# Layer 0 of a graph transformer: two PSUM banks become one region that scores, weights and picks share in turn

## The chip, the cores and the metric

The kernel runs on one core of one Trainium2 chip. A core has five engines that work side by side, each through its own queue in order: PE (TensorE, matmuls; PEld is its weight load), DVE (VectorE), ACT (ScalarE), POOL (GpSimd) and SP (SyncE, which here only issues DMAs). PE writes its results into PSUM, which has eight banks of 128 partitions x 512 fp32 values, and DVE or ACT copy them out. The metric is the device time of one execution in microseconds (us), lower is better.

## The reference

Three layers of graph attention over 6250 nodes of 64 features and 206250 edges that are sorted by target node; then a log-softmax, a residual and a layer norm:

```python
q = x @ Wq + bq;  k = x @ Wk + bk;  v = x @ Wv + bv
e = edge_attr @ We
alpha = sum(q[dst] * (k[src] + e)) / sqrt(64)          # one score per edge
p = exp(alpha - segment_max(alpha, dst)[dst])
w = p / segment_sum(p, dst)[dst]
agg = segment_sum((v[src] + e) * w, dst)
x = relu(agg + x @ Ws + bs)                            # layers 0 and 1: then a layer norm
```

## The kernel before, in words

Edges are cut into chunks of 768 (six tiles of 128), and four chunks make a unit: 67 full units and a rest. A unit's edges meet only a few target nodes, 32 for each chunk, so its scores are one 128 x 768 matrix: four groups of 32 rows (one for each chunk) by 768 edges, computed in two halves of 384 columns.

For a unit, each layer does this:
- **Gather.** The features of each edge's source node are needed. Most come by indirect DMA (POOL, L607). Some tiles come from PE instead, as *picks*: edges are sorted so that a tile's sources lie in known windows of nodes, and a matmul of a one-hot matrix `hot` (made on DVE from keys, L1342) with the node features `parts` picks them out (L1404, eight matmuls of 256 columns for one tile of two chunks). Each pick gives four candidates side by side in PSUM. DVE copies the first out (L1365) and overwrites it with the second, third and fourth where a mask says so (L1367, three `COPY_PREDICATED`). This is `evacuate()`. A later `swap()` on ACT (L1353 to L1355) exchanges lower halves between the two chunks.
- **Turn.** Features are transposed on PE (L1705) and copied by ACT to `featT` (L1708), one chunk in each quarter of the unit.
- **Scores** (`products`, L1718): PE multiplies `featT` with the queries. **Most** (L1732): DVE adds the mask and keeps the row maximum. **Powers** (L1751): ACT takes the exponential over both halves. **Weights** (L1765): PE transposes the result, three tiles for each half, and ACT copies it out (L1768). **Sums** (L1777): PE multiplies the weights with the features, and ACT copies the result out (L1784).

Layer 0 has a second job beside this, the sorter: it brings the edges of each unit into the order that the picks need. A unit of sorting is 12 steps, called by `move(n)`. Each step makes two `hit` matrices on DVE (L1081) for the step after next, prepares a third of the edge data on DVE (L1049 or L1052), and does six matmuls with them on PE (L1092), in half of the steps four more (L1101), with transposes (L1135) in four of the steps. Every fourth unit a `mark` runs beside it for about two units: it computes the positions of the next 16 chunks, almost all on DVE (L916 to L1017) with a few matmuls (L930, L949, L951, L977, L1006). A group of 512 nodes that is complete is finished and projected for the next layer in small pieces at the start of units (for instance L1449 on PE, L1451 on DVE, L1554 on PE, L1557 on DVE).

The order on each engine is the order in which the loop over units writes the instructions; nothing reorders it. In one pass `u` of that loop, unit `u` is turned quarter by quarter (`j` = 0 to 3), unit `u-1` gets scores, most, powers and weights, unit `u-2` gets sums, and picks are made for unit `u+1`. With eight tiles from picks a unit of layer 0 has four picks, one in each quarter: two sorter steps, the pick, one more step, `evacuate()`.

PSUM in layer 0 before: tag `a` has two banks (transposes and the sorter's small things), `x` two (the sorter's products), `g`, `m`, `s` and `p` one each. Bank `s` holds scores half 0, scores half 1, the pick of quarter 1 and the pick of quarter 2 in turn. Bank `p` holds the pick of quarter 0, weights half 0, weights half 1 and the pick of quarter 3. Each tenant starts when the last has been read out. Layers 1 and 2 have other pools (opened after layer 0), where picks already come in doubles, with copies of 256 columns, in two buffers of two banks.

In the listings the same work has other numbers after the change: scores L1723 for L1718, most L1737 for L1732, the negated maximum L1750 for L1745, powers L1756 for L1751, weights L1776 for L1765, probT L1779 for L1768, sums L1788 for L1777. Lines up to L1404 keep theirs.

## Time and profile before

| what | value |
|---|---|
| median of 3 runs | 4164.22 us (4156.0 to 4164.31) |
| the profiled execution | 4160.32 us, of which the span is 4158.5 us |
| PE busy | 3390.2 us (82%) |
| DVE busy | 3094.5 us (74%) |
| POOL busy | 2819.2 us (68%) |
| ACT busy | 2344.7 us (56%) |
| mean granted clock of PE | 0.925 |

A row of the timeline gives the start (us from the span's start), the time of the group (us), engine, line, operation, output<-inputs with partitions x elements, the count, and in brackets how long the engine sat idle before it and what ended that. Starts of PE's matmuls are denser than their times, since they are pipelined. A row of the windows gives a stretch, its length, and the busy time and instructions of PE, PEld, DVE, ACT and POOL in it, then the granted clock, the share of the DMA engines and GB/s.

### The profile page before, as it was taken

The page shows a single profiled execution, that of the slowest core. Times are in us where ns is not written, and L with a number is a line of the kernel's source. Part 1 is how long each engine was busy: PE and PEld are TensorE (multiplying, and loading weights), DVE is VectorE, ACT ScalarE, POOL GpSimd, SP SyncE. Part 2 cuts the span into 40 slices and gives each one's busy share as a digit, 9 for nine tenths or more (in the row PEclk, how much of TensorE's full clock was granted, in tenths as well). Part 3 has the DMA queues.
Part 4 walks back from the last instruction along what each step waited for, and adds up shares of the span by engine and source line. Part 5 has one row for each costly group of instructions (what it writes and reads, how often), then busy time and mean ns, then how long its engine had stood idle before and what let it go on. Part 6 is the DMA issues. An engine that isn't in the chain of part 4 may idle for free.

```text
span 4158.5 us, 105258 instructions
## 1 busy us (share of the span) xinstructions
PE 3390.2 (82%) x34183; PEld 2406.9 (58%) x34183; DVE 3094.5 (74%) x10306; ACT 2344.7 (56%) x5994; POOL 2819.2 (68%) x2774
## 2 busy tenths in 40 slices
PE   3779988998999899995778788888758788787776
PEld 2345555555555555553666666666646666666664
DVE  5678888888888888874566677677646767777775
ACT  1345555555565565563555556665535666666665
POOL 5466666666666666663777777777747777777774
PEclk9889999999999999996899999999969999999997
DMA  5657676667667767675677777777657677777774
GB/s 120 165 163 194 175 186 177 168 181 185 174 176 186 181 174 187 171 199 137 151 181 185 189 191 188 185 190 197 167 129 183 176 185 186 185 185 190 185 185 100
DMA packets 787997, 728.88 MB, mean 175 GB/s; under 512 B 487336, under 2 KB 612450, under 8 KB 787440
## 3 DMA queue, kind: packets, MB, share of 16 engines
q1 hardware_dynamic: 630436, 504.14, 47.5%
q0 software_dynamic: 88448, 90.75, 11.8%
q10 hardware_dynamic: 68556, 127.16, 8.6%
q8 instruction: 278, 4.55, 0.5%
q14 instruction: 279, 2.29, 0.2%
HBM read 562.78 MB, written 158.81 MB: 174 GB/s over the span
## 4 chain that ended last, share of the span: by engine, by line


## 5 line engine op out<-in xcount | busy, mean ns | idle before, releaser
L607 POOL DMA_INDIRECT feat<-x,gate x1592 | 1568.8, 985 | 485.3 <-issue 367.3
L607 POOL DMA_INDIRECT feat<-in_x,gate x1100 | 1177.7, 1071 | 676.0 <-ACT gate L639 360.8
L1404 PE MATMUL ps_x<-parts,hot 128*128 128x256 f32 x6336 | 942.5, 301 | 0.0
L1404 PEld LDWEIGHTS ps_x<-parts,hot 128*128 128x128 f32 x6336 | 842.2, 202 | 82.2 <-DVE feat L1367 65.6
L1708 ACT COPY featT<-ps_a 64x384 f32<-64x384 f32 x1320 | 626.7, 475 | 410.3 <-PE ps_a L1705 392.7
L1367 DVE COPY_PREDICATED feat<-which,ps_x 128x256 f32<-128x256 int32 (+1 forms) x1584 | 592.8, 374 | 54.3
L1365 DVE COPY feat<-ps_x 128x256 f32<-128x256 f32 (+1 forms) x528 | 187.8, 356 | 580.8 <-PE ps_x L1404 564.9
L1705 PE MATMUL ps_a<-ident,feat 128*128 128x128 f32 x2380 | 450.2, 290 | 145.2 <-DMA feat<-x,gate 107.0
L1705 PEld LDWEIGHTS ps_a<-ident,feat 128*128 128x128 f32 x2380 | 285.1, 145 | 354.1 <-issue 261.1
L1081 DVE TENSOR_SCALAR hit<-ruler,pos 128x384 bf16<-128x384 f16 x1608 | 457.3, 326 | 7.3 <-PE ps_m L1101 6.6
L1342 DVE TENSOR_SCALAR hot<-keys,rank 128x512 fp32r<-128x512 f16 (+1 forms) x1040 | 432.7, 483 | 5.4 <-DMA keys<-keyS 5.4
L1777 PE MATMUL ps_p<-feat,probT 128*32 128x128 f32 x6600 | 242.8, 300 | 84.6 <-ACT probT L1768 73.8
L1092 PE MATMUL ps_x<-hit,raw 128*64 128x384 bf16 x1608 | 296.0, 364 | 0.5 <-DVE hit L1081 0.4
L1092 PE MATMUL ps_x<-hit,rest 128*64 128x384 bf16 x1608 | 277.8, 342 | 0.0
L1092 PE MATMUL ps_x<-hit,end 128*64 128x384 bf16 x1608 | 277.3, 341 | 0.0
L1777 PEld LDWEIGHTS ps_p<-feat,probT 128*32 128x32 f32 x6600 | 198.9, 122 | 123.2 <-ACT probT L1768 98.2
L1718 PE MATMUL ps_s<-featT,q 128*32 128x384 f32 x1866 | 235.2, 509 | 32.6 <-DVE most L1732 25.4
L1765 PE MATMUL ps_s<-ident,prob 128*128 128x128 f32 (+1 forms) x417 | 83.4, 313 | 215.4 <-ACT prob L1751 214.3
L1751 ACT ACTIVATE prob<-prob,part 128x768 f32<-128x768 f32 x204 | 190.0, 932 | 83.8 <-DVE part L1745 75.5
L1125 ACT COPY eT<-ps_x 128x384 f32<-128x384 f32 x268 | 129.3, 483 | 122.5 <-PE ps_x L1092 89.6
L1765 PEld LDWEIGHTS ps_s<-ident,prob 128*128 128x128 f32 (+1 forms) x417 | 47.8, 152 | 245.9 <-ACT prob L1751 241.5
L1143 ACT COPY feat<-ps_a 128x384 f32<-128x384 f32 x256 | 122.1, 481 | 120.6 <-PE ps_a L1135 89.7
(280 smaller groups left out, 6019.1 us busy)
## 6 DMA issues: line engine op xcount, KB each, us to landing
featT<-eaS SPq DMA_DIRECT2D x658, 192.0 KB
feat<-eaP SPq DMA_DIRECT2D x134, 768.0 KB
raw<-in_ea SPq DMA_DIRECT2D x536, 96.0 KB
eaS<-eT ACTq DMA_DIRECT2D x134, 384.0 KB
keys<-keyS SPq DMA_DIRECT2D x132, 384.0 KB
eaP<-feat ACTq DMA_DIRECT2D x128, 384.0 KB
shade<-maskS SPq DMA_DIRECT2D x198, 192.0 KB
fourth<-eaS SPq DMA_DIRECT2D x134, 192.0 KB
```

Source lines behind the costliest of these rows:

```text
L607: nc.gpsimd.indirect_dma_start(out=feat[:, c, t, 0], out_offset=None, in_=xts[layer][:, :], in_offset=bass.IndirectOffsetOnAxis(ap=index[: ...
L1081: nc.vector.tensor_scalar(hit, ruler, self.pos[:, at : at + 1], None, ALU.is_equal)
L1092: nc.tensor.matmul(self.px[j * D : (j + 1) * D, :HE], self.parts[2 * h + i].thirds[part][:, j, t * D : (t + 1) * D], self.hits[h, 2 * i + ...
L1342: nc.vector.tensor_scalar(hot[:, h], keys[self.layer, k][:, first : first + n], rank[:, h : h + 1], None, ALU.is_equal)
L1365: nc.vector.tensor_copy(found, px[:, :, :, 0])
L1367: nc.vector.copy_predicated(found, which[:, :, :, b].bitcast(I32).unsqueeze(3).to_broadcast([P, 2, m, D]), px[:, :, :, b],)
L1404: nc.tensor.matmul(px[:, t - t0, v].rearrange("p b d -> p (b d)"), hot[:, h, (2 * pair + v) * P : (2 * pair + v + 1) * P], those[:, i, b0 ...
L1705: nc.tensor.transpose(pt[:, t * P : (t + 1) * P], rows[:, 2 * t * D : 2 * (t + 1) * D], ident)
L1708: nc.scalar.copy(featT[:, :, h, :], pt[h * D : (h + 1) * D, : n * P].rearrange("d (i e) -> d i e", e=P))
L1718: nc.tensor.matmul(p_s[rows, :w], self.q[:, rows], self.featT[j][:, cols], start=True, stop=True)
L1751: nc.scalar.activation(self.prob[:n, : self.cols], self.prob[:n, : self.cols], AF.Exp, bias=neg, accum_out=self.part[:n, P + 1 : P + 2],)
L1777: nc.tensor.matmul(p_g[rows, :].rearrange("n (h d) -> n h d", h=2), self.probT[:, t, rows], batch[:, j, t], start=(t == 0), stop=(t == sel ...
```

## The change

The two banks `s` and `p` of layer 0 become one region `sp` of two neighbouring banks, of which there is one. In turn it holds: both halves of the scores, a double pick, both halves of the weights, a double pick. So in one pass of the loop both halves of the scores are computed at its start, both maxima are taken on DVE after the first sorter step, both halves of the weights are transposed at the start of quarter 2, and there are two double picks, in quarters 1 and 3, in place of four single ones. Each quarter now runs one sorter step, the pick, one step, `evacuate()`, one step. Matmuls, their number and their shapes stay the same. The copies of a pick on DVE are half as many and twice as wide. Layers 1 and 2 are not touched.

```diff
-    bank_of = {"node": "g", "s0": "s", "s1": "s", "w0": "p", "w1": "p"}
+    bank_of = {"node": "g"}
...
-        wide = 2 if len(psum) > 1 and tag == "x" else 1
+        wide = 2 if tag == ("x" if len(psum) > 1 else "sp") else 1
...
-            room = 2 if self.layer else 1
+            room = 2
...
-                bank = "x" if self.layer else "pssp"[self.quarter]
+                bank = "x" if self.layer else "sp"
...
         def scores(self, h):
-            p_s = ps(f"s{h}")
+            if len(psum) > 1:
+                p_s = ps(f"s{h}")
+            else:
+                if not h:
+                    self.pair = ps("sp")
+                p_s = self.pair[:, h * 512 : (h + 1) * 512]
...
         def weights(self, h):
-            p_t = ps(f"w{h}")[:, : m * P].rearrange("p (t n) -> p t n", t=m)
+            if len(psum) > 1:
+                p_t = ps(f"w{h}")
+            else:
+                if not h:
+                    self.pair = ps("sp")
+                p_t = self.pair[:, h * 512 : (h + 1) * 512]
+            p_t = p_t[:, : m * P].rearrange("p (t n) -> p t n", t=m)
...
             line.products(u - 1, 0)
+            if not layer:
+                line.products(u - 1, 1)
...
                 if j == 2 and not layer:
                     line.weights(u - 1, 0)
+                    line.weights(u - 1, 1)
...
                 a, b = -(-n * j // LB), -(-n * (j + 1) // LB)
+                if not layer:
+                    a, b = n * j // LB, n * (j + 1) // LB
...
                 if not layer:
-                    move(pace - pace // 2)
+                    move(pace // 3)
                     if j == 0:
                         line.most(u - 1, 0)
+                        line.most(u - 1, 1)
                     for _ in range(b - a):
                         next(picking, None)
-                    move(pace // 2)
+                    move(pace // 3)
                     picker.evacuate()
+                    move(pace // 3)
                 if j == 0:
-                    if not layer:
-                        line.products(u - 1, 1)
-                        if not placed(0, u + 1):
-                            line.most(u - 1, 1)
-                            line.powers(u - 1)
```

How this moves instructions, at three places. First PE, at the start of a pass (`stamp` are the last matmuls of the sorter step, L1777 the sums, `featT,q` the scores, `ident,feat` the turn of quarter 0, `keyc` the first small matmul of the sorter's index). Before:

```order
L1101 MATMUL ps_m<-hit,stamp_266 32x384
L1777 MATMUL ps_g<-feat,probT 32x128 x24
L1718 MATMUL ps_s<-featT,q 32x384 x4
L1705 MATMUL ps_a<-ident,feat 128x128 x3
L1172 LDWEIGHTS keyc
```

And now:

```order
L1101 MATMUL ps_m<-hit,stamp_266 32x384
L1788 MATMUL ps_g<-feat,probT 32x128 x24
L1723 MATMUL ps_sp<-featT,q 32x384 x8
L1705 MATMUL ps_a<-ident,feat 128x128 x3
L1172 LDWEIGHTS keyc
```

The second half of the scores has moved ahead of quarter 0's turn and of the index matmuls (L1172, L1174). Second, DVE in quarter 0 of a pass in which a mark begins (L916 to L926 are the mark's first pieces, the two ISA rows of a line are the mask and maximum of one half, `hit` the sorter's matrices). Before:

```order
L916 TENSOR_TENSOR spare<-src_b,bound 128x1536
L1081 TENSOR_SCALAR hit<-ruler,pos 128x384 x2
L1052 TENSOR_TENSOR end<-rest 128x384
L923 TENSOR_TENSOR kinds<-spare 128x1440
L924 TENSOR_TENSOR flags<-spare 128x384
L925 TENSOR_TENSOR flags<-flags 128x192
L926 TENSOR_TENSOR spare<-flags 128x3x32
L1732 ISA prob,most<-ps_s,shade 128x384
L1732 ISA most 128x1
L1081 TENSOR_SCALAR hit<-ruler,pos 128x384 x2
L1365 COPY feat<-ps_p 128x2x64
L1367 COPY_PREDICATED feat<-which,ps_p 128x2x64 x3
```

And now:

```order
L916 TENSOR_TENSOR spare<-src_b,bound 128x1536
L1737 ISA prob,most<-ps_sp,shade 128x384
L1737 ISA most 128x1
L1737 ISA prob,most<-ps_sp,shade,most 128x384
L1737 ISA most 128x1
L1750 TENSOR_SCALAR part<-most 128x1
L1081 TENSOR_SCALAR hit<-ruler,pos 128x384 x2
L1052 TENSOR_TENSOR end<-rest 128x384
L923 TENSOR_TENSOR kinds<-spare 128x1440
```

Both maxima now stand one step earlier, and quarter 0 has no pick to copy out. Third, DVE at the end of quarter 3 of that pass (L970 is a piece of the mark, `which` the masks for the next unit's picks, made at the pass's end). Before:

```order
L970 TENSOR_TENSOR spare<-spare 128x96
L1081 TENSOR_SCALAR hit<-ruler,pos 128x384 x2
L1365 COPY feat<-ps_p 128x2x64
L1367 COPY_PREDICATED feat<-which,ps_p 128x2x64 x3
L1331 TENSOR_TENSOR which<-kbs,four 128x64
```

And now:

```order
L970 TENSOR_TENSOR spare<-spare 128x96
L1365 COPY feat<-ps_sp 128x2x128
L1367 COPY_PREDICATED feat<-which,ps_sp 128x2x128 x3
L1081 TENSOR_SCALAR hit<-ruler,pos 128x384 x2
L1331 TENSOR_TENSOR which<-kbs,four 128x64
```

The copies of the pick have moved ahead of the last step's `hit` matrices, and are 256 columns wide (2 chunks x 128). On ACT the swaps move from quarters 0 and 2 to quarters 1 and 3, and the two copies of weights stand together at the start of quarter 2. The order on SP and POOL is the same but for line numbers.

More of the change, by code (lines that the diff above doesn't have):

```diff
@@ L1718, in scores @@
                 nc.tensor.matmul(p_s[rows, :w], self.q[:, rows], self.featT[j][:, cols], start=True, stop=True)
-            self.scored = p_s
+            self.scored = [p_s] if not h else self.scored + [p_s]
         def most(self, h):
@@ L1724, in most @@
             w = cols.stop - cols.start
-            p_s = self.scored
+            p_s = self.scored[h]
             if h and self.plain and self.k >= NT:
@@ L1977, in main_path @@
                     line.begun()
-                    if not layer and placed(0, u + 1):
-                        line.most(u - 1, 1)
+                    if not layer:
                         line.powers(u - 1)
                 a, b = -(-n * j // LB), -(-n * (j + 1) // LB)
+                if not layer:
+                    a, b = n * j // LB, n * (j + 1) // LB
                 if layer:
@@ L1991, in main_path @@
                 if not layer:
-                    move(pace - pace // 2)
+                    move(pace // 3)
                     if j == 0:
                         line.most(u - 1, 0)
+                        line.most(u - 1, 1)
                     for _ in range(b - a):
                         next(picking, None)
-                    move(pace // 2)
+                    move(pace // 3)
                     picker.evacuate()
+                    move(pace // 3)
                 if j == 0:
-                    if not layer:
-                        line.products(u - 1, 1)
-                        if not placed(0, u + 1):
-                            line.most(u - 1, 1)
-                            line.powers(u - 1)
                     ask(layer, u + 1)
@@ L2008, in main_path @@
                 if j == 2:
-                    line.weights(u - 1, 0 if layer else 1)
+                    if layer:
+                        line.weights(u - 1, 0)
                     if not this.placed:
```

2 lines of the change are left out of this document (1 added, 1 removed).

## The prediction

> **What bounds the kernel now.** I read the page's slices, then windows unit by unit, then the timeline of one unit of each kind, then the waits inside them.
>
> ```profile
> PE   3779988998999899995778788888758788787776
> DVE  5678888888888888874566677677646767777775
> ```
>
> Layer 0 is the first 18 slices of 104 us. PE and DVE are both above 80% there, so the share names no bound. Windows from one pass's sums to the next do:
>
> ```profile
> 985.39:1014.08 28.69, 24.79 (x255) 14.18 (x247) 27.12 (x92) 15.44 (x40) 22.38 (x19) 1.00 0.77 213
> 1014.08:1042.97 28.89, 24.16 (x245) 14.78 (x246) 25.10 (x94) 14.79 (x42) 13.36 (x15) 0.94 0.57 143
> 1042.97:1065.26 22.29, 22.29 (x238) 13.39 (x234) 20.02 (x65) 15.06 (x39) 17.03 (x17) 1.00 0.74 193
> 1065.26:1087.55 22.29, 21.68 (x241) 13.56 (x237) 19.89 (x70) 15.03 (x39) 16.71 (x17) 1.00 0.79 218
> ```
>
> The pattern repeats every fourth unit. Two passes carry a mark: DVE is busy 27.1 of 28.7 us, then 25.1 of 28.9. Two are plain: PE is busy 22.3 of 22.3, and 21.7 of 22.3. So plain passes are PE's. The marked ones are DVE's, as its waits from 988.5 to 1032.4 us show:
>
> ```profile
> DVE src_b L1182 <- PE ps_g L1174: 0.4, 1, 0.4
> ...
> L916 DVE TENSOR_TENSOR spare<-src_b,bound x17: 1722/2244/2267, 50.4 to 1730.5; 128x1536 bf16<-128x1536 int32 x16, 128x1152 bf16<-128x1152 int32 x1
> ```
>
> In 44 us DVE waits once, 0.4 us. L916 opens a mark; the first of 17 lies before the loop, so there are 16 such pairs of passes.
>
> **The cost of a pick's copies.** The wide form is not in layer 0, but layers 1 and 2 run it from a region of two banks:
>
> ```profile
> L1367 DVE COPY_PREDICATED feat<-which,ps_p 128x128 f32<-128x128 int32 x372 | 112.7, 303 | 12.8
> L1365 DVE COPY feat<-ps_p 128x128 f32<-128x128 f32 x124 | 35.3, 285 | 34.0 <-PE ps_p L1404 32.6 <-issue 1.0
> L1367 DVE COPY_PREDICATED feat<-which,ps_x 128x256 f32<-128x256 int32 x792 | 353.7, 447 | 27.1
> L1365 DVE COPY feat<-ps_x 128x256 f32<-128x256 f32 x264 | 111.6, 423 | 224.5 <-PE ps_x L1404 223.0 <-issue 0.6
> ```
>
> A single is 0.285 + 3 x 0.303 = 1.19 us, a double 0.423 + 3 x 0.447 = 1.76 us, so a double saves 2 x 1.19 - 1.76 = 0.62 us of DVE. With 60 units of four picks (eight tiles each) that is 120 doubles, 74 us of DVE. It counts only where DVE sets the pace.
>
> **Plain passes.** PE does the same matmuls, so nothing is gained there but a few changes between kinds of matmul, which I cost at nothing. The question is whether the single region makes PE wait. The PE and DVE rows of a plain pass:
>
> ```profile
> 1077.04 1.21 PE L1404 MATMUL ps_s<-parts,hot 128*128 128x256 f32 x8
> 1078.08 0.49 PE L1135 MATMUL ps_a<-ident,eT 128*128 128x128 f32 x3
> 1079.39 0.55 PE L1765 MATMUL ps_p<-ident,prob 128*128 128x128 f32 x3
> 1086.76 0.35 PE L1092 MATMUL ps_x<-hit,raw 128*64 128x384 bf16 x2
> 1087.55 1.48 PE L1777 MATMUL ps_g<-feat,probT 128*32 128x128 f32 x48
> 1088.86 0.82 PE L1718 MATMUL ps_s<-featT,q 128*32 128x384 f32 x8
> 1089.61 0.55 PE L1705 MATMUL ps_a<-ident,feat 128*128 128x128 f32 x3
> 1078.28 0.29 DVE L1365 COPY feat<-ps_s 128x128 f32<-128x128 f32 x1 [0.49 <-PE ps_s L1404]
> 1086.87 0.29 DVE L1365 COPY feat<-ps_p 128x128 f32<-128x128 f32 x1 [0.51 <-PE ps_p L1404]
> ```
>
> - Weights (quarter 2) now wait for the pick of quarter 1 to be copied out. Before, PE reached them 1079.39 - 1078.28 = 1.11 us after DVE could start, behind one sorter step. Now two steps lie between; one takes 1079.39 - 1078.08 = 1.31 us, so PE arrives 2.42 us after. The copies take 1.76: 0.66 us to spare.
> - Scores now wait for the pick of quarter 3. They came 1088.86 - 1086.87 = 1.99 us after; one more step adds 1087.55 - 1086.76 = 0.79: 2.78 against 1.76, 1.02 us to spare.
> - DVE waited 0.5 us for each of these picks, so it is early, and has less to do before them now.
> - The pick of quarter 1 waits for the maxima, which stand a whole quarter ahead of it; the pick of quarter 3 waits for ACT's two copies of weights, with a turn and three steps between. ACT is busy 15 of 22 us; the swap that joins powers in quarter 1 has 5 us of picks and steps as cover. If that cover went, it would cost PE at most its own three copies, about 1 us a pass.
>
> Plain passes: 0.
>
> **First marked pass.** DVE's stretch starts when the index matmuls (L1174) land, and ends, for the next pass, with the mark's flags (L963), which release PE's L977 and the sums behind it. Rows of the pair:
>
> ```profile
> 988.58 0.20 DVE L1182 TENSOR_TENSOR src_b<-ps_g,shift 128x24 int32<-128x24 f32 x1 [0.40 <-PE ps_g L1174]
> 1013.58 0.20 DVE L963 TENSOR_SCALAR flags<-spare 128x96 bf16<-128x96 f32 x1
> 1013.81 0.19 PE L977 MATMUL ps_a<-flags,tri 128*128 128x32 bf16 x1 [0.97 <-DVE flags L963]
> 1015.24 0.68 DVE L1081 TENSOR_SCALAR hit<-ruler,pos 128x384 bf16<-128x384 f16 x2
> 1015.41 0.83 PE L1718 MATMUL ps_s<-featT,q 128*32 128x384 f32 x8
> 1017.76 0.63 PE L1449 MATMUL ps_a<-ident,y 128*64 128x128 f32 x4 [1.05 <-ACT featT L1708]
> 1018.75 0.68 DVE L1451 COPY xT<-ps_a 64x512 f32<-64x512 f32 x1
> 1029.59 0.55 PE L1135 MATMUL ps_a<-ident,eT 128*128 128x128 f32 x3 [1.73 <-ACT featT L1708]
> 1030.95 1.76 PE L1404 MATMUL ps_s<-parts,hot 128*128 128x256 f32 x8
> 1032.75 0.29 DVE L1365 COPY feat<-ps_s 128x128 f32<-128x128 f32 x1 [0.29 <-PE ps_s L1404]
> ```
>
> Between 988.58 and 1013.58 lie the picks of quarters 0, 1 and 2: three singles become one double, 3 x 1.19 - 1.76 = 1.81 us less. Against it, L1174 now stands behind the second half of the scores too, 1089.61 - 1088.86 = 0.75 us, and DVE waits for it there already. Net 1.06 us. PE's waits grow in this pass (weights behind the copies), but DVE has mark pieces meanwhile and needs PE only several steps later.
>
> **Second marked pass.** DVE does one double (end of the first marked pass) in place of two singles (that one and quarter 0's): -0.62 us. But scores wait for it. The copies start where the `hit` row stood, 1015.24, and end at 1017.00, against scores at 1015.41: PE starts them 1.6 us later, and they last 0.75 us longer. Where a group's projection stands in that pass, DVE then waits: L1449, 2.35 us behind the scores' start, comes at 1017.00 + 2.35 + 0.75 = 20.1, ends 20.7, and DVE is free for L1451 at 1018.75 + 0.57 = 19.3. That is 1.4 us, from nothing before. Such a piece stands in about half of these passes (my estimate from the order): +0.7. The two cancel: +0.1.
> In quarter 1 the pick now stands ahead of the step on which PE stalled 1.73 us, so DVE no longer waits for it (0.29 us before), and the copies come one step earlier. PE's weights then wait for the end of the copies. What that is worth lies between nothing (PE leaves the quarter as late as before, now behind the copies) and the 1.73 us of the stall; since the copies of 1.76 us take the place of a pick of 1.21 us and its wait, it is nearer to nothing, and I take 0.4. Net of the pass 0.3 us.
>
> **The sum.** 16 x (1.06 + 0.3) = 22 us less. The last passes, after the sorter has ended, have no steps to cover the region's turns:
>
> ```profile
> L1732 DVE CUSTOM_DVE_ANT_0 prob<-ps_s,shade,most 128x384 f32<-128x384 f32 x65 | 40.0, 615 | 12.4 <-PE ps_s L1718 12.0
> L1732 DVE CUSTOM_DVE_ANT_0 prob<-ps_s,shade 128x384 f32<-128x384 f32 x67 | 37.2, 556 | 9.5 <-PE ps_s L1718 8.0
> ...
> L1768 ACT COPY probT<-ps_p 128x384 f32<-128x384 f32 x84 | 41.1, 489 | 27.5 <-PE ps_a L1705 10.8 <-PE ps_p L1765 8.6 <-DMA keys<-keyS 7.3
> ...
> 1852.60:1869.27 16.67, 12.85 (x141) 9.18 (x133) 8.50 (x32) 12.22 (x32) 11.48 (x13) 1.00 0.73 209
> 1869.27:1883.83 14.56, 10.43 (x119) 8.00 (x119) 9.85 (x34) 8.12 (x23) 11.21 (x12) 1.00 0.55 123
> ```
>
> One turn of the region there is scores (2 x 0.75), maxima (0.56 + 0.62), two picks of 16 matmuls (2 x 2 x 1.04, from the rows at 1077.04 and 1078.08) with their copies (2 x 1.76), and ACT's two copies of weights (2 x 0.49): 11.4 us with no cover at all, less than the 14.6 us of the shorter of these passes. I take 0 (bounds -1 and +4 us). Layers 1 and 2 follow layer 0 in time, so its gain is the kernel's. 4160.3 - 22 = 4138 us. That execution lies 3.9 us below the median of the runs, 0.1%, inside the 0.2% that this kernel's measurement can tell.
>
> [...]
>
> **Rivals.**
> - *All of DVE's saving arrives* (0.15): the marked passes drop by more, since stalls of PE on DVE shorten with it. For it: the largest wait of PE in layer 0's middle,
>
> ```profile
> PE ps_s L1718 <- DVE most L1732: 16.9, 18, 3.6
> ```
>
>  is for the maximum of half 0 and vanishes with joined scores. Against: most of it lies in DVE's own stretch. Up to 74 us; I price it at 60: 4100.
> - *PE waits for the region in plain passes too* (0.25): the point is DVE reaching the copies more than 0.66 us (weights) or 1.02 us (scores) after the pick ends. Then each further microsecond is PE's. With 32 plain passes and 0.7 us exposed at each of two places, 45 us, less the 22: 4183. For it: DVE is busy 20 of 22 us in these passes and must make `hit` and `rest` beside the longer copies. Against: it waited 0.5 us at each pick.
> - *The longer PE waits lower the clock* (0.15): the second marked pass has 0.94 of the clock, so 0.06 x 28.9 = 1.7 us, and its pick takes 1.76 against 1.21 us after a stall of 1.73. Now PE stalls about 2 us in both marked passes. One more such stretch in a pass that PE bounds, 16 x 1.7 = 27, less the 22: 4165, no change. [...]
>
> **How the numbers follow.** Forecast 0.45 (4120 to 4152 alone), rivals 0.15, 0.25, 0.15. Faster by over 0.2%: 0.45 + 0.15 = 0.60; same 0.15; slower 0.25. The range reaches from the first rival to the second: 4098 to 4185.
>
> **What would show it.** Right: windows of marked pairs shorter by 1 to 2 us, plain passes still 22.3 us with PE full; L1365 and L1367 on `ps_sp` at 0.42 and 0.45 us; no wait of L1723 or L1776 for L1367 in plain passes, some 1 to 2 us in marked ones. Wrong: plain passes above 23 us with PE waiting for L1367, or clock below 1.00 in them.

## The result, and the profile after

The changed kernel takes 4259.96 us (median, 4253.64 to 4264.13). The kernel before, run beside it, takes 4160.11 us. The ratio is 1.0238, with a 95% interval of 1.0222 to 1.0254. The forecast was 4138 us, so the sign was wrong, and the time lies above the range. The traces below are of executions of 4160.32 and 4253.64 us, 93 us apart where the medians are 100 apart.

The loss is in layer 0 alone. Windows of both kernels, cut where layer 0's last sums start, before first:

```profile
0.00:1920.20 1920.20, 1656.96 (x16302) 984.94 (x16302) 1590.43 (x5615) 1043.36 (x2697) 1202.34 (x1134) 0.95 0.67 175
1920.20:4158.50 2238.30, 1733.26 (x17881) 1421.95 (x17881) 1504.11 (x4692) 1301.33 (x3298) 1616.87 (x1640) 0.91 0.70 176
```

```profile
0.00:2021.51 2021.51, 1677.73 (x16302) 1015.24 (x16302) 1539.08 (x5135) 1050.68 (x2697) 1176.79 (x1134) 0.93 0.64 166
2021.51:4251.90 2230.39, 1719.18 (x17881) 1401.65 (x17881) 1505.71 (x4692) 1302.35 (x3298) 1614.46 (x1640) 0.92 0.69 177
```

Layer 0 grew by 101.3 us and the rest shrank by 7.9. DVE did 51.4 us less in layer 0, as the change intends. PE sat idle longer, 2021.51 - 1677.73 = 343.8 us against 263.2, and its same 16302 matmuls took 20.8 us more (1677.73 against 1656.96).

The same four passes as in the prediction, after:

```profile
1028.76:1060.52 31.76, 27.26 (x254) 15.54 (x246) 27.79 (x90) 14.88 (x39) 20.33 (x19) 0.89 0.65 175
1060.52:1090.24 29.72, 24.59 (x246) 15.56 (x247) 23.25 (x80) 15.54 (x44) 13.59 (x14) 0.94 0.55 144
1090.24:1113.13 22.89, 21.94 (x238) 13.41 (x234) 18.85 (x57) 15.20 (x39) 17.30 (x16) 1.00 0.76 197
1113.13:1136.02 22.89, 21.33 (x240) 13.56 (x236) 18.47 (x62) 15.10 (x39) 17.14 (x16) 1.00 0.80 212
```

Each is longer than its counterpart (28.69, 28.89, 22.29, 22.29). Nine such groups in a row, before and after:

```profile
669.57:1614.07 944.50, 859.71 (x8736) 518.24 (x8732) 839.73 (x2952) 557.10 (x1450) 621.15 (x577) 0.96 0.69 180
```

```profile
698.28:1693.25 994.97, 865.48 (x8733) 530.41 (x8728) 811.01 (x2664) 561.17 (x1450) 603.48 (x576) 0.95 0.65 171
```

That is 50.5 us for nine groups, 5.6 each. By the windows of the single passes, the means rose by 2.4 us for the first marked pass (30.84 to 33.26), 1.0 for the second (28.65 to 29.66), and 1.1 for each plain one (22.4 to 23.5, 23.1 to 24.2). Of the 50.5 us, 44.7 are idle time of PE (84.8 to 129.5) and 5.8 are slower matmuls. What PE waits for in the middle of layer 0 (650 to 1750 us; total, times, longest), after:

```profile
PE ps_sp L1776 <- ACT probT L1779: 40.0, 40, 2.1
PE ps_a L930 <- DVE kinds L923: 39.6, 10, 5.5
...
PE ps_m L1101 <- ACT mask L1160: 9.4, 8, 1.4
PE ps_x L1092 <- DVE hit L1081: 8.8, 9, 1.5
```

Of these, only the second stood among the larger waits of the kernel before:

```profile
PE ps_a L930 <- DVE kinds L923: 16.0, 10, 2.8
```

**The first wait: weights for ScalarE.** PE's and ACT's rows in a plain pass, after:

```profile
1099.47 2.15 PE L1404 MATMUL ps_sp<-parts,hot 128*128 128x256 f32 x16
...
1104.12 0.55 PE L1776 MATMUL ps_sp<-ident,prob 128*128 128x128 f32 x3
1105.62 0.55 PE L1776 MATMUL ps_sp<-ident,prob 128*128 128x128 f32 x3 [0.95 <-ACT probT L1779]
1105.07 0.50 ACT L1779 COPY probT<-ps_sp 128x384 f32<-128x384 f32 x1
```

PE transposes the first half of the weights, and the next three transposes start only when ACT's copy of that half has ended (1105.57). The halves lie in different banks, but in one tile, and `weights(0)` issues its copy before `weights(1)` issues its transposes. So the second half waits for a reader of the first, 0.95 us here, and 0.87 to 2.05 us in all 40 passes between 650 and 1750 us. The plain pass grew by 0.60; the other 0.35 us came back, and where was not looked into.

**The second wait: kinds for the maxima.** In the first marked pass, DVE's rows and then PE's, after:

```profile
1036.04 0.56 DVE L1737 CUSTOM_DVE_ANT_0 prob<-ps_sp,shade 128x384 f32<-128x384 f32 x1
...
1036.64 0.62 DVE L1737 CUSTOM_DVE_ANT_0 prob<-ps_sp,shade,most 128x384 f32<-128x384 f32 x1
...
1037.38 0.54 DVE L1081 TENSOR_SCALAR hit<-ruler,pos 128x384 bf16<-128x384 f16 x2
...
1038.30 0.90 DVE L923 TENSOR_TENSOR kinds<-spare 128x1440 bf16<-128x1440 bf16 x1
```

```profile
1035.68 0.33 PE L1092 MATMUL ps_x<-hit,end 128*64 128x384 bf16 x2
1039.26 1.36 PE L930 MATMUL ps_a<-kinds,ones 128*1 128x480 bf16 x3 [3.25 <-DVE kinds L923]
...
1042.92 3.26 PE L1404 MATMUL ps_sp<-parts,hot 128*128 128x256 f32 x16
```

And before, where the maximum stood behind the kinds:

```profile
992.91 0.92 DVE L923 TENSOR_TENSOR kinds<-spare 128x1440 bf16<-128x1440 bf16 x1
993.88 0.77 PE L930 MATMUL ps_a<-kinds,ones 128*1 128x480 bf16 x3 [1.28 <-DVE kinds L923]
```

From 1036.04 to 1037.38 DVE works on the two maxima while PE has nothing to do; the hits and the kinds follow. PE's wait grew from 1.28 to 3.25 us. Counted from the start of the pass, PE is ready for L930 at the same point as before (7.25 us, before 7.21), and the kinds end 2.0 us later (10.44, before 8.44): 1.34 us for the maxima, and 0.64 because the index matmuls now stand behind the second half of the scores (DVE's L1182 starts after 3.83 us, before 3.19).

Behind the wait PE's matmuls are slower for some 7 us: L930 takes 1.36 us against 0.77, and the double pick 3.26, against 2.15 in the plain pass. The granted clock is 0.55 from 1039.26 to 1046.02, and 1.00 from the start of the pass to the wait. Over the whole pass it is 0.89, where it was 1.00; in the mean of the nine first marked passes it is 0.91, where it was 0.95. DVE then waits for the slowed pick, which ends at 1042.92 + 3.26 = 1046.18 (the profile names a DMA, but the copy starts when the pick ends):

```profile
1046.21 0.42 DVE L1365 COPY feat<-ps_sp 128x256 f32<-128x256 f32 x1 [1.04 <-DMA feat<-in_x,gate]
```

DVE, which had waited once, 0.4 us, in the 44 us of the marked pair that the prediction shows, waits six times in the same stretch now, 5.1 us in all. Over the middle of layer 0 (650 to 1750 us) its waits for the picks are no longer than before; the waits for the sorter's matmuls are new. The largest, before and then after:

```profile
DVE feat L1365 <- PE ps_s L1404: 28.6, 43, 1.6
DVE feat L1365 <- PE ps_p L1404: 18.4, 30, 1.7
```

```profile
DVE feat L1365 <- PE ps_sp L1404: 46.5, 52, 1.7
DVE hit L1081 <- PE ps_m L1101: 35.9, 42, 1.7
DVE rest L1049 <- PE ps_x L1092: 31.9, 30, 2.0
```

**The second marked pass.** The same two maxima stand ahead of the mark's next pieces there. ACT waits for one of these (L991) and has the sorter's mask behind it, for which PE waits in its turn:

```profile
1072.93 0.27 ACT L992 CAST misc<-spare 128x96 bf16<-128x96 int32 x1 [3.26 <-DVE spare L991]
1073.11 0.47 ACT L1160 CAST mask<-ps_m 128x384 bf16<-128x384 f32 x1
1073.63 0.35 PE L1101 MATMUL ps_m<-hit,stamp 128*32 128x384 bf16 x4 [1.41 <-ACT mask L1160]
```

All eight of PE's waits for the mask at L1101 (9.4 us above) lie in second marked passes; the kernel before has none in that stretch. ACT's wait for L991 is 3.3 us in the mean of the nine passes, before 2.2.

**The copies.** Their price held. Groups of the wide form on `ps_sp`:

```profile
L1367 DVE COPY_PREDICATED feat<-which,ps_sp 128x256 f32<-128x256 int32 x360 | 160.6, 446 | 12.3
...
L1365 DVE COPY feat<-ps_sp 128x256 f32<-128x256 f32 x120 | 50.9, 424 | 110.6 <-PE ps_sp L1404 96.8 <-DMA feat<-in_x,gate 7.6 <-issue 5.3
```

### The profile page after: what moved, and what is told of

Its sections match the earlier page's. It is cut to its first block, busy times and chain, and to the rows that moved or that the text cites. A ratio compares the mean times of both kernels' runs of the same rounds, so it can differ in the third digit from the quotient of the medians.

```text
span 4251.9 us, 104850 instructions
## 1 busy us (share of the span) xinstructions
PE 3396.9 (80%) x34183; PEld 2416.9 (57%) x34183; DVE 3044.8 (72%) x9826; ACT 2353.0 (55%) x5994; POOL 2791.3 (66%) x2774
## 3 DMA queue, kind: packets, MB, share of 16 engines
q0 software_dynamic: 88448, 90.75, 11.4%
## 4 chain that ended last, share of the span: by engine, by line
## 5 line engine op out<-in xcount | busy, mean ns | idle before, releaser
L607 POOL DMA_INDIRECT feat<-in_x,gate x1100 | 1152.1, 1047 | 796.1 <-ACT gate L639 446.8
L1367 DVE COPY_PREDICATED feat<-which,ps_x 128x256 f32<-128x256 int32 (+1 forms) x1584 | 593.0, 374 | 54.4
L1705 PE MATMUL ps_a<-ident,feat 128*128 128x128 f32 x2380 | 462.1, 293 | 177.5 <-DMA feat<-x,gate 135.6
L1081 DVE TENSOR_SCALAR hit<-ruler,pos 128x384 bf16<-128x384 f16 x1608 | 443.9, 323 | 54.4 <-PE ps_m L1101 54.4
L1092 PE MATMUL ps_x<-hit,raw 128*64 128x384 bf16 x1608 | 299.2, 363 | 12.3 <-DVE hit L1081 11.7
L1404 PE MATMUL ps_sp<-parts,hot 128*128 128x256 f32 x1952 | 289.9, 305 | 1.3 <-DVE most L1737 1.3
L1092 PE MATMUL ps_x<-hit,rest 128*64 128x384 bf16 x1608 | 281.4, 343 | 0.0
L1092 PE MATMUL ps_x<-hit,end 128*64 128x384 bf16 x1608 | 278.6, 343 | 0.0
L1404 PEld LDWEIGHTS ps_sp<-parts,hot 128*128 128x128 f32 x1952 | 264.0, 207 | 23.6 <-issue 21.5
L1125 ACT COPY eT<-ps_x 128x384 f32<-128x384 f32 x268 | 129.5, 483 | 119.6 <-PE ps_x L1092 89.2
```

Source lines behind the costliest of these rows:

```text
L607: nc.gpsimd.indirect_dma_start(out=feat[:, c, t, 0], out_offset=None, in_=xts[layer][:, :], in_offset=bass.IndirectOffsetOnAxis(ap=index[: ...
L1081: nc.vector.tensor_scalar(hit, ruler, self.pos[:, at : at + 1], None, ALU.is_equal)
L1092: nc.tensor.matmul(self.px[j * D : (j + 1) * D, :HE], self.parts[2 * h + i].thirds[part][:, j, t * D : (t + 1) * D], self.hits[h, 2 * i + ...
L1125: nc.scalar.copy(halves(self.eT[i]), spread(self.px))
L1367: nc.vector.copy_predicated(found, which[:, :, :, b].bitcast(I32).unsqueeze(3).to_broadcast([P, 2, m, D]), px[:, :, :, b],)
L1404: nc.tensor.matmul(px[:, t - t0, v].rearrange("p b d -> p (b d)"), hot[:, h, (2 * pair + v) * P : (2 * pair + v + 1) * P], those[:, i, b0 ...
```

## The experiments

All edits ran on five Trainium2 chips on which the kernel before takes 1.34 to 1.36 times as long as on the chip of the result, 5574 to 5647 us at a granted clock of PE near 0.83 (there 0.925), and the changed kernel, on the one where it ran, 1.35 times (5739.95 us). So only ratios to the kernel before on the same chip are compared. Two kernels that ran on two chips each gave 1.0090 and 1.0098, and 1.0074 and 1.0076. The first four edits' expectations were written in microseconds for the first chip; 4160 us is 1.000 and the changed kernel 1.024.

The changed kernel and the kernel before, as controls:

> The changed kernel itself, to stand beside the edits on the same chip. 1.022 to 1.026 of the kernel before if the chip is like the one of the first result; on a chip where every kernel is slower (the first four edits ran where the kernel before took 5647 us) the ratio is 1.02 to 1.04, since the edits with one cause less measured 1.016 and 1.021 there.

> The kernel before itself, for its trace on a chip where every kernel is slower. Ratio 1.000 within 0.003. If VectorE still set the marked passes there, its share in them is over 0.9 as in the first trace; if TensorE does, at a clock near 0.83, VectorE is below 0.8 in them and the 50 us that the doubles save buy little.

Measured: 1.0278 (1.0241 to 1.0315), and 1.0000 (0.9987 to 1.0013). The loss there is of the size of the first chip's. It is layer 0's too; the first stretch of the windows, kernel before and then changed (on another of the chips):

```profile
0.00:2435.23 2435.23, 1904.55 (x16302) 1084.50 (x16303) 1592.84 (x5615) 1047.72 (x2697) 1182.80 (x1134) 0.88 0.52 138
```

```profile
0.00:2601.86 2601.86, 1966.25 (x16302) 1152.20 (x16302) 1536.33 (x5135) 1054.87 (x2697) 1134.24 (x1134) 0.85 0.49 129
```

DVE is busy 65% of layer 0 in the kernel before there (1592.84 of 2435.23), against 83% on the first chip. In the marked passes between 937 and 1970 us it is busy 69 to 87% of the first and 73 to 81% of the second. So DVE has slack in these passes there that it had not on the first chip, and the experiments test the waits under another balance of the engines. The two waits of the changed kernel (650 to 2300 us):

```profile
PE ps_sp L1776 <- ACT probT L1779: 87.1, 41, 4.0
PE ps_a L930 <- DVE kinds L923: 43.5, 11, 5.5
```

### Each wait alone, and both

In `weights`, both halves' transposes ahead of both copies:

```diff
-            nc.scalar.copy(self.probT[:, t0 : t0 + m, :n], p_t[:, :, :n])
+            self.turning = ([] if not h else self.turning) + [(t0, m, p_t)]
+            if h or len(psum) > 1:
+                for t0, m, p_t in self.turning[0 if len(psum) == 1 else h :]:
+                    nc.scalar.copy(self.probT[:, t0 : t0 + m, :n], p_t[:, :, :n])
```

> The changed kernel, with one thing moved: the transposes of both halves of the weights are issued before the two copies to probT, so TensorE's second three transposes no longer stand behind ScalarE's copy of the first half in the shared region. Theory A (that wait is a good part of the loss): the row of TensorE at the transposes waiting for ScalarE's probT (40 us in 40 waits over 650 to 1750 us of the changed kernel's trace) goes, the plain passes fall from 22.9 us back to about 22.3, and with some 32 plain passes at 0.6 us and the marked ones at 0 to 0.95 us the time falls by 20 to 50 us, to 4210 to 4240. Theory B (the loss is the place of the maxima alone, the wait only takes up slack): 4250 to 4262.

The second maximum back at the second step:

```diff
                 if j == 1:
...
+                        line.most(u - 1, 1)
                         line.powers(u - 1)
...
                     if j == 0:
                         line.most(u - 1, 0)
-                        line.most(u - 1, 1)
```

> The changed kernel, with the second maximum put back where the kernel before has it: at the start of the second step of the pass instead of right behind the first maximum. Theory B (both maxima and their small operation stand ahead of VectorE's hits and kinds, TensorE waits for these, its clock falls, and the marked passes become longer): the first marked pass of four falls by 1.5 to 3.3 us and the time by 25 to 60 us, to 4200 to 4235. Theory A (only the wait of the transposes counts): 4250 to 4265. Against both: the region is then held by the scores until the second step, so a pick of that step could wait for it and the time could rise by 5 to 20 us.

Both edits:

> The changed kernel with both edits: transposes of both halves ahead of the two copies, and the second maximum back at the second step. If the two causes are separate the gains add: 4160 to 4195. If they are one (a TensorE late at one place waits less at the other), the time is that of the better edit alone, 4200 to 4235. A time below 4150 would say that the joined region with double picks is worth something once its two waits are gone.

> The changed kernel with both edits (transposes of both halves ahead of the two copies; second maximum back at the second step), once more. If the two waits are the cause: 0.010 to 0.018 below the ratio of the changed kernel beside it, that is 1.004 to 1.014 of the kernel before. If they are not, it stays within 0.005 of the changed kernel.

| kernel | ratio | 95% interval |
|---|---|---|
| changed | 1.0278 | 1.0241 to 1.0315 |
| transposes ahead of copies | 1.0161 | 1.0135 to 1.0187 |
| second maximum apart | 1.0206 | 1.0181 to 1.0232 |
| both (two chips) | 1.0090, 1.0098 | 1.0059 to 1.0121, 1.0067 to 1.0130 |

The first edit takes off 0.0117 alone and 0.0116 on top of the second (1.0206 to 1.0090). The second takes off 0.0072 alone and 0.0071 on top of the first. The figures for one edit alone compare two chips (the changed kernel ran on a chip on which the single edits did not); those on top of the other edit, and 1.0278 to 1.0098 for both, are each from one chip. So the causes are two, and they add: theories A and B each hold a part. The second edit alone lies in neither range of its expectation, and both together at 1.0090, between the two ranges written for them; those ranges started from a loss of 0.024, which here is 0.028. With the first edit alone the wait for probT is no longer among the larger ones, and the one for the kinds stays. With the second the wait for probT stays, and the one for the kinds falls from 43.5 to 24.7 us, near the 19.7 us of the kernel before there. Their rows, first edit and then second:

```profile
PE ps_a L930 <- DVE kinds L923: 40.6, 11, 5.5
```

```profile
PE ps_sp L1776 <- ACT probT L1779: 95.5, 37, 4.2
PE ps_a L930 <- DVE kinds L923: 24.7, 8, 4.5
```

Together they explain two thirds of the loss there: 0.0278 becomes 0.0094.

### Both maxima late

On top of both edits, the first maximum too goes behind the first step's pieces:

```diff
                 if j == 1:
...
+                        line.most(u - 1, 0)
                         line.most(u - 1, 1)
                         line.powers(u - 1)
...
-                    if j == 0:
-                        line.most(u - 1, 0)
```

> The edit with both waits removed, and now the first maximum too at the second step, so both stand together but behind the first step's hits and pieces. If what costs is the maxima's place ahead of the first step's work on VectorE: 1.003 to 1.009. If the powers, the weights and the picks that follow the maxima are late instead (their reader is the exponential, and six transposes stand behind it): 1.010 to 1.025.

> The changed kernel with both waits removed and both maxima at the second step, once more. On a chip where the kernel before takes 5600 us: 1.005 to 1.010 as before. On a chip where it takes 4160 us: the two waits there are 0.6 us in each plain pass and 2 to 3 us in each first marked pass; if they carry the loss, 1.000 to 1.008, against 1.0238 for the changed kernel.

Measured 1.0074 (1.0050 to 1.0099) and 1.0076 (1.0053 to 1.0100), about 0.002 better; the intervals overlap with those of both edits, so this small gain is not certain. The powers and weights behind the maxima did not suffer. PE's wait for the mask at L1101, 15.8 us in the changed kernel and 8.1 and 8.8 with both edits, is 4.7 and 4.8 us here, so that wait too goes with the place of the maxima. The larger waits then:

```profile
PE ps_sp L1776 <- DVE feat L1367: 28.7, 19, 3.1
PE ps_a L930 <- DVE kinds L923: 24.9, 12, 3.9
```

### The pieces around the picks

Three edits move the sorter's pieces. In the kernel before, only the pieces and the picks' places of the change:

```diff
+                if not layer:
+                    a, b = n * j // LB, n * (j + 1) // LB
...
-                    move(pace - pace // 2)
+                    move(pace // 3)
...
-                    move(pace // 2)
+                    move(pace // 3)
                     picker.evacuate()
+                    move(pace // 3)
```

> The kernel before with only the sorter's pieces and the picks' places of the changed kernel: one piece ahead of the pick, one ahead of its copies, one behind; picks rounded down to the later steps. Single picks, scores and weights as before. Theory E (what is left of the loss with both waits gone lies here): 1.004 to 1.012. Theory F (it lies with the double picks in a region that all four uses share): 0.994 to 1.002.

Measured 1.0012 (0.9991 to 1.0033): this part of the change costs nothing that can be told. In that run PE waits 82.8 us at the picks for probT, where the kernel before has 38.9 us, and the time does not follow: here the longer wait was no lost time. On top of both edits, the order of before (two pieces, pick, one piece, copies):

> The edit with both waits removed, with the pieces of the sorter around the picks as in the kernel before: two pieces ahead of the pick and one between it and its copies, in place of one, one and one behind the copies. If the place of the copies ahead of the last piece matters (TensorE's next pick or transposes wait for the region): 1.010 to 1.016. If the copies come too early so that VectorE waits for a slow pick, giving it one piece more ahead helps: 1.003 to 1.009.

And on top of the late maxima, the pick first (pick, two pieces, copies, one piece):

> The edit with both waits removed and both maxima late, with the pick right behind the step, ahead of all three pieces, and its copies behind two of them. If the pick gets to TensorE earlier and the copies stand farther behind it, so that VectorE waits less for the pick: 0.3 to 1 per cent below e9 beside it. If the pick then pushes TensorE's work for the sorter's pieces back by its 2.2 us: 0.3 to 1.5 per cent above.

Measured 1.0205 (1.0169 to 1.0240) and 1.0187 (1.0138 to 1.0236), 0.011 worse each than what they were built on. One wait grew in both. In the order of before, and then in the same kernel with the pieces of the change (on another of the chips):

```profile
PE ps_sp L1776 <- DVE feat L1367: 70.5, 33, 4.6
```

```profile
PE ps_sp L1776 <- DVE feat L1367: 9.0, 11, 3.1
```

With a piece between the copies and the weights, PE hardly waits for the region (17.0 us in the other run of that kernel); without it, it waits 33 times. In the second of the two (pick first) the same wait is 67.1 us, though a piece still stands behind the copies. There the pick itself waits for the maxima, 37.4 us in 35 times where the kernel it is built on has 5.7 us, and both pieces that stand ahead of the copies come behind the pick on PE. Which of the two costs the time was not taken apart.

### One part alone in the kernel before

> The kernel before with only the scores put together: second half's scores behind the first half's at the start of the pass (into the second of the two banks), both maxima behind the first step, the powers at the second step. Single picks and weights as before. Theory B (the maxima ahead of the kinds and hits make the first marked pass longer by 1.5 to 3.3 us): 16 passes give 25 to 55 us, ratio 1.006 to 1.013. Theory C (the place of the maxima costs nothing; what costs is the shared region with the double picks): 0.998 to 1.003.

> The kernel before with only the weights put together: transposes of both halves at the start of the third step, into the two separate banks, copies between as in the changed kernel. Since the halves lie in two tiles here, the second three transposes wait for no copy. Theory A (the wait for ScalarE in the shared tile is what the joined weights cost): no change, 0.998 to 1.003. If putting six transposes and two copies in one place costs by itself (ScalarE's copies stand ahead of the masks and the converted pieces that TensorE needs next): 1.004 to 1.010.

Measured 1.0315 (1.0277 to 1.0352) and 1.0120 (1.0083 to 1.0157), above what any theory gave, though the interval of the second reaches down into its last range. Both edits had to share out the two banks anew, and brought waits of their own, so they answer less than they were meant to. With scores together, the first quarter's single pick follows the second maximum in bank `p`:

```profile
PE ps_p L1404 <- DVE most L1732: 137.4, 42, 7.2
```

With weights together, the first half follows a pick in `s`, and the third quarter's pick follows the weights:

```profile
PE ps_s L1765 <- DVE feat L1367: 28.9, 15, 3.3
PE ps_s L1404 <- ACT probT L1768: 17.0, 16, 1.8
```

With the halves in two tiles no transpose of weights waits for ACT's copy (between 650 and 2300 us), so that wait does hang on the one tile. What they show besides is that in these two kernels a PSUM tenant that came sooner behind another paid for it, without any shared tile (137.4, 28.9 and 17.0 us above).

### What is left: the region and the doubles

Doubles with scores and weights taken one half at a time, each half holding the region in its turn; then the same with the scores together; then weights one half at a time with the scores together and both maxima late:

```diff
-                if not h:
-                    self.pair = ps("sp")
-                p_t = self.pair[:, h * 512 : (h + 1) * 512]
+                p_t = ps("sp")
...
                 if j == 2 and not layer:
                     line.weights(u - 1, 0)
-                    line.weights(u - 1, 1)
...
                 if j == 2:
-                    if layer:
-                        line.weights(u - 1, 0)
+                    line.weights(u - 1, 0 if layer else 1)
```

> Double picks with copies of 256 columns in the joined region, but scores and weights one half at a time as in the kernel before: each half takes the whole region in its turn, the second scores at the end of the first step, the second maximum at the second step, the second weights at the end of the third step. Theory D (putting the halves together costs, the doubles alone gain): 0.985 to 0.998 of the kernel before. Rival: the region has one buffer where there were two banks, so TensorE waits at each turn for the reader before (0.5 to 1 us, some four turns a pass): 1.005 to 1.02.

> The changed kernel with the second maximum at the second step and the weights one half at a time at their places of before; only the scores' matmuls stay together, beside the doubles. If the place of the weights matters (the weights together in separate banks cost 1.2% by themselves), it lies 0.003 to 0.012 below the edit with both waits removed (1.009), that is at 0.997 to 1.006. If only the wait for ScalarE's copy mattered, it lies at 1.007 to 1.012.

> The changed kernel with both maxima at the second step and the weights one half at a time at the places of before, each with the region to itself. If the place of the weights holds the rest of the loss: 0.998 to 1.004. If the rest lies with the region that four uses share, and not with where the weights stand: 1.005 to 1.010, as e9.

Measured 1.0098 (1.0073 to 1.0122), 1.0077 (1.0055 to 1.0100) and 1.0032 (1.0015 to 1.0049). The first of these answers a rival that the two waits alone leave open. With nothing put together, doubles in one region still lose 0.0098, inside the range for PE waiting at each turn of the region and not in that of theory D (a gain); its larger waits are for probT, 44.8 us, and for the kinds, 31.9 us. So part of the loss does not need the halves to be put together: a single region that changes hands more often has it too. Scores' matmuls may stay together (1.0077 is not above 1.0098). The weights' two places are worth 0.004 beside the late maxima (1.0075 to 1.0032); beside the early first maximum they are worth 0.002 (1.0094 to 1.0077), which the intervals do not tell from nothing. This is the best version, and it is still slower than the kernel before: none beats it.

Last, what the doubles are worth. Single picks in the region of the changed kernel, and double picks with copies of 128 columns on top of the late maxima (the cut is of this second edit; the first sets `room` to 1 in layer 0):

```diff
-            nc.vector.tensor_copy(found, px[:, :, :, 0])
...
+            alone = 1 if not self.layer else m
+            for i in range(0, m, alone):
+                one = slice(i, i + alone)
+                nc.vector.tensor_copy(found[:, :, one], px[:, :, one, 0])
...
```

> The changed kernel with picks one by one again (a pick of 8 matmuls and copies of 128 columns), in the joined region: the 50 us of VectorE's work that the doubles save come back. If VectorE's work still sets the marked passes, the time rises by 15 to 50 us, to 4275 to 4310. If VectorE now only waits for TensorE in the time saved, it stays within 10 us of 4260; if doubles themselves do harm (TensorE works 2.2 us or more on a double while the hits' matmuls stand behind it), it falls to 4210 to 4245.

> The edit with both waits removed and both maxima late (1.0075), with double picks but copies of 128 columns again: eight narrow copies in place of four wide ones, 0.62 us more VectorE for each of some 120 doubles, 74 us in all. If VectorE's work is on the path of the marked passes: 1.012 to 1.018. If the saving buys nothing where TensorE sets the pace: 1.007 to 1.010.

Measured 1.0390 (1.0360 to 1.0420), which is 0.011 above the changed kernel, and 1.0118 (1.0089 to 1.0146), 0.0043 above the version with wide copies. The first does not price the copies: with four picks in the region, PE waits 125.3 us at the picks for the maxima. The second does, on another chip than the versions it is compared with; the three intervals overlap at their ends (1.0089 to 1.0146 against 1.0050 to 1.0099 and 1.0053 to 1.0100). So the wide copies probably save time even where DVE is busy only 62% of layer 0 (1532.74 of 2484.86, the version with wide copies):

```profile
0.00:2484.86 2484.86, 1921.59 (x16302) 1121.50 (x16303) 1532.74 (x5135) 1045.71 (x2697) 1170.52 (x1134) 0.87 0.51 135
```

0.0043 of 5583 us is 24 us out of 74 us of copies saved. With the narrow copies PE's wait for the copies at the weights (L1367, here L1370) is longer than the 28.7 us shown above:

```profile
PE ps_sp L1779 <- DVE feat L1370: 53.3, 31, 4.5
```

That is 24.6 us more, about the whole difference. So the gain may come as a shorter turn of the region rather than as DVE's time in the marked passes; it was not tested, and the longer wait of the pieces alone cost no time.

What stays open: 0.0032 of the loss, and how the loss of the first chip divides. There the waits are shown by the trace, and that the same edits would take off the same shares there was not run.

## Why the prediction was wrong, point by point

- **What bounds the kernel before.** That PE is the bound in plain passes held: they are longer by what PE waits. That the marked passes are DVE's held for the kernel before, and not after the change: in the second marked pass DVE's work fell from 25.10 to 23.25 us and the pass still grew to 29.72.
- **The cost of a pick's copies.** Right: 0.424 and 0.446 us after, against 0.423 and 0.447 taken. That the 22 us of the sum lie near the 24 us of the experiment is chance: they were DVE's time in marked passes that it bounds, and the experiment ran where it does not bound them. It is the other terms that failed.
- **"Plain passes: 0."** This step failed. The spare of 0.66 and 1.02 us was right: in the middle of layer 0 no wait of scores or weights for L1367 is among PE's larger ones. But I looked at the turns from one tenant to the next, and not inside one: second half behind the copy of the first, 0.95 us, net 0.60 in the passes shown. The text had "at most its own three copies, about 1 us a pass" as the price of the swap losing its cover; that the wait inside the weights costs nearly the same is chance. Part of the rest of the mean 1.1 us lies in plain passes where DVE finishes a group of nodes and the maxima delay the hits: there PE's L1092 waits up to 1.5 us for L1081. Neither sign that the text named for this case came: in the plain passes shown the clock is 1.00 and they take 22.89 us, and in none does PE's wait for L1367 show among the larger ones.
- **"First marked pass", -1.06.** Failed, and by the most: +2.4. The step at fault is "DVE has mark pieces meanwhile and needs PE only several steps later". It priced what PE's lateness does to DVE, and left out what DVE's lateness does to PE: both maxima, 1.34 us (1036.04 to 1037.38), were moved ahead of the hits and the kinds, and I costed that move at nothing. PE then waits 3.25 us, its clock is 0.55 for the next 6.8 us, and DVE waits 1.04 us for the slowed pick. On the slower chips, moving one maximum back took off 0.0072.
- **"Second marked pass", -0.3.** Failed in sign, +1.0. The sum held the copies against the scores and left out the same move of the maxima: PE waits 0.95 us inside the weights here too, and up to 1.41 us for the sorter's mask, behind the mark's pieces that the maxima delay. The stall of 1.73 us that the text counted on is gone, but these two waits are in its place.
- **Last passes, 0 with bounds -1 and +4.** Failed: the first two took 16.67 and 14.56 us, and now

```profile
1944.88:1964.96 20.08, 14.88 (x140) 11.99 (x132) 6.34 (x23) 12.07 (x31) 12.63 (x14) 0.83 0.54 157
1964.96:1984.02 19.06, 11.98 (x120) 10.02 (x119) 9.35 (x26) 8.81 (x25) 14.12 (x15) 0.91 0.37 82
```

 which is 7.9 us more, at clocks of 0.83 and 0.91 where it was 1.00. The argument that one turn of 11.4 us fits into a pass of 14.6 took the turn as the only thing in the pass. No run takes these passes apart.
- **The sum by these.** 16 x (2.4 + 1.0 + 1.1 + 1.1) = 90 us, and 8 us for the last passes: 98, against 101.3 in layer 0.
- **The rivals.** *PE waits for the region in plain passes too* had the right sign and a time still 77 us below the measured one. Its mechanism, DVE late to the copies, is not what happened, so the sign came by another way; that the mechanism is real shows where a piece was taken away behind the copies (0.011 slower, PE's wait 9.0 or 17.0 to 70.5 us). *The longer PE waits lower the clock* happened in the first marked pass (0.89 against 1.00), right behind the wait for the kinds: 5.8 us of nine groups' 50.5 are longer matmuls. *All of DVE's saving arrives* did not: PE took its place as the bound.
- **The turns and the clock.** I took each turn from one tenant to the next as covered by the sorter's steps, which it is in the passes shown (PE has no wait for L1367 between 650 and 1750 us); the wait of 0.95 us is inside one tenant, between halves that do lie in different banks. As to the clock, the trace shows matmuls 1.5 to 1.8 times as long behind an idle time of 3.25 us (3.26 to 2.15, 1.36 to 0.77), but also behind one of 1.97 us (ending at 1478.50; L1092 then takes 0.53 us against 0.33) and, in the kernel before, behind the 1.73 us of the prediction's row (a pick of 1.76 against 1.21). Behind waits of 1.41 and 0.53 us a double pick took 2.17 us in one second marked pass (start 743.42) and 3.78 in another (1517.31). So no single idle time separates the slow stretches from the others here. What holds is the count: in the nine groups L930 took over 1 us in eight first marked passes after the change, and in three before.

## What to carry to other kernels

When two buffers become one, look for waits within a tenant as well as between tenants: the second of two writes into one tile waited for the read between them, 0.87 to 2.05 us each time, though the two touch different banks. Put all writes first (on top of the second edit this took 1.0206 to 1.0090). When an operation moves on the engine that seems to be the bound, list what stands behind it on that engine and which other engine waits for that, before costing the move at nothing: DVE did 51.4 us less in layer 0 here, and the layer took 101.3 us more.

## What was not expected of the hardware

On three of the later chips PE spends stretches of several us in which its matmuls start one or a few at a time, some 0.7 or 1.4 us apart, and wait for nothing that the profile shows. Sums, in the edit with the transposes first, which has 158.0 us in 241 such waits of its sums between 650 and 2300 us:

```profile
982.76 0.27 PE L1791 MATMUL ps_g<-feat,probT 128*32 128x128 f32 x1 [0.74 <-issue]
983.49 0.27 PE L1791 MATMUL ps_g<-feat,probT 128*32 128x128 f32 x1 [0.46 <-issue]
...
985.65 0.27 PE L1791 MATMUL ps_g<-feat,probT 128*32 128x128 f32 x1 [1.15 <-issue]
```

The kernel before has it there as well, 148.4 us in 235 such waits, and five more of the edits 92.3 to 166.6 us. On the first chip the changed kernel has one wait of PE that nothing in the profile ends between 650 and 1750 us, of 0.4 us, and none at the sums. Why these chips differ was not found out; the instructions and their order are the same.
